# Attention's output projection in two halves with a PSUM bank of its own, and three PSUM banks instead of four for the values

## The chip, the cores and the metric

The kernel runs on one core of a Trainium2 chip. The metric is the time of one execution on the device in microseconds (us); lower is better. The core's engines are called as the profile calls them: PE is TensorE (PEld its weight loads), DVE is VectorE, ACT is ScalarE, POOL is GpSimd and SP is SyncE. PSUM, where matmuls write, has eight banks, each of 512 fp32 numbers on 128 partitions.

## The reference, cut to what matters

The input is an image of 256 x 256 places with 32 channels. Four layers follow one another, each of the form x = x + f(group_norm(x)): a gated attention, two Sobel filters (smoothing, two gradients, the root of the sum of their squares) and a recurrent network of two cells over 256 steps. The change lies in the first layer:

```python
mn = (m - mu) * jax.lax.rsqrt(var + LN_EPS) * ln_gamma + ln_beta
v = (mn @ Wv).reshape(B, s, i, H, C)                 # 32 -> 256 channels
g = jax.nn.sigmoid(mn @ Wg).reshape(B, s, i, H, C)   # 32 -> 256 channels
a = jnp.einsum('bsihc,btihc->bstih', q, k) * C ** (-0.5)
a = jax.nn.softmax(a, axis=2)
o = g * jnp.einsum('bstih,bsihc->bsihc', a, v)
return o.reshape(B, s, i, H * C) @ Wo + bo           # 256 -> 32 channels
```

In the last einsum `a` is summed over t, over which the softmax sums to one, so that o = g * v: what has to be computed is v, g, their product, and the projection with Wo.

## The kernel before, in words

The whole image stays on the chip. `xa` holds it with 128 partitions (four neighbouring columns of the image x 32 channels), 64 blocks of 256 places; two blocks make a pair, one operand of 128 x 512. `xb` has the normalized input of the attention in the same layout. There are NST = 32 pairs, and the attention runs over them in the step variable i.

In a step, `u` takes two values, 2i and 2i + 1: the halves of the 256 channels of v and g. In each half there are four values of `j`, the column within the group of four, which are 32 partitions each. So a step has eight value matmuls (Wv, line 313, into `pv`) and eight gate matmuls (Wg, line 313, into `pg`), each with 32 rows of contraction, 128 output channels and 512 places: each takes one of four row parts of TensorE, and different parts can work side by side. A sigmoid on ACT (line 328) turns a gate into `sg`, and a multiply on DVE (line 331) makes the product `o` from a value in PSUM and its gate.

`together` emits a group of four matmuls, two values and then two gates for later values, on four different row parts; after them the two sigmoids and the two multiplies. A half of a step has two such groups, and a step four. The gates run ahead: the first group of a half makes the gates of the next half's j = 2, 3, the second those of j = 0, 1 of the half after that, as the loop below has it.

`project(i)` (lines 333 to 347) makes the output of step i from its eight products: four matmuls for each half of the 256 channels (line 337), each with 128 rows of contraction and 32 output channels, one for each 32 partitions of the result, summed over the two halves in one bank `po`. Then ACT adds the bias (line 345, into `r`), POOL adds it to `xa` (line 347), and, two steps later, DVE takes the statistics of the new `xa` for the next normalization (line 350).

The order of instructions on each engine is the order in which the program emits them (`manual_schedule`). The eight PSUM banks are split into two pools of four: `ps_v` for the values, and `ps_g` for the gates and `po`. A tile takes over a bank of its pool when what was in it before has been read.

```python
for i in range(NST):
    for u in (2 * i, 2 * i + 1):
        if i >= 3 and u % 2:
            statistics(i - 3)
        together([(u, 0), (u, 1)], [(u + 1, 2), (u + 1, 3)])
        together([(u, 2), (u, 3)], [(u + 2, 0), (u + 2, 1)])
    if i >= 1:
        project(i - 1)
```

After the loop come the projection of the last step, the last three statistics and the normalization for the Sobel layer.

Of the kernel before, what the change touches and what calls it, by code (L numbers as in the profile page):

```python
# [10 lines left out]
F32 = mybir.dt.float32  # L11
# [3 lines left out]
PSUM = bass.MemoryType.PSUM  # L15

S = 256
T = 256
C = 32
J = 4  # L20
NB = T // J
P = 128
# [36 lines left out]
def net_kernel(  # L59
# [20 lines left out]
    nc = tc.nc  # L80
# [47 lines left out]
    wo = cp.tile([P, D // P, C], F32, name="wo")  # L128
    nc.gpsimd.dma_start(out=wo, in_=w_o.rearrange("(k p) c -> p k c", p=P))

    NST = NB // 2
    one = eps_tile(1.0, "one")

    def table(func, after):

        t = small.tile([P, 1], F32, name="table")
        nc.scalar.activation(t, after, func, scale=0.0, bias=one)
# [56 lines left out]
    with tc.tile_pool(name="nat", bufs=3) as natp, tc.tile_pool(  # L194
        name="ps_in", bufs=4, space=PSUM
# [33 lines left out]
    def pair(t, k):  # L229
        return t[:, 2 * k : 2 * k + 2, :].rearrange("p b s -> p (b s)")  # L230

    with tc.tile_pool(name="ln", bufs=4) as lnp:
        rstd = lnp.tile([P, 2 * S], F32, name="rstd", bufs=1)
        with tc.tile_pool(name="ps_ln", bufs=6, space=PSUM) as ps_ln, tc.tile_pool(
            name="ps_var", bufs=1, space=PSUM
# [38 lines left out]
        with tc.tile_pool(name="ps_sp", bufs=8, space=PSUM) as ps_sp:  # L274
            for i, (k, g, ks) in enumerate(pairs):
# [4 lines left out]
                    lhsT=spread[rows, ks * J : (ks + 1) * J, :].rearrange("p j c -> p (j c)"),  # L280
                    rhs=rstd[rows, :],
                    start=True,
                    stop=True,
# [18 lines left out]
    stats = new_stats()  # L302
    with tc.tile_pool(name="at", bufs=3) as atp, tc.tile_pool(
        name="ps_g", bufs=4, space=PSUM
    ) as ps_g, tc.tile_pool(name="ps_v", bufs=4, space=PSUM) as ps_v:
        gates, gated = {}, {}

        def inner(w, u, j, ps):
            i, half = divmod(u, 2)
            k = pairs[i][0]  # L310
            rows = slice(j * C, (j + 1) * C)
            mn = xb[rows, 2 * k : 2 * k + 2, :].rearrange("p b s -> p (b s)")
            nc.tensor.matmul(  # L313
                ps, lhsT=w[rows, half * P : (half + 1) * P], rhs=mn, start=True, stop=True
            )
            return ps

        def together(values, gates_of):

            pvs = {k: inner(wv4, *k, ps_v.tile([P, 2 * S], F32, name="pv")) for k in values}  # L320
            pgs = {
                k: inner(wg4, *k, ps_g.tile([P, 2 * S], F32, name="pg"))
                for k in gates_of
                if k[0] < 2 * NST
            }
            for k, pg in pgs.items():
                gates[k] = sg = atp.tile([P, 2 * S], F32, name="sg", bufs=8)
                nc.scalar.activation(sg, pg, AF.Sigmoid)  # L328
            for k, pv in pvs.items():
                gated[k] = o = atp.tile([P, 2 * S], F32, name="o", bufs=17)  # L330
                nc.vector.tensor_mul(o, pv, gates.pop(k))  # L331

        def project(i):
            po = ps_g.tile([P, 2 * S], F32, name="pg")
            for half in range(2):
                for j in range(J):
                    nc.tensor.matmul(
                        po[j * C : (j + 1) * C, :],
                        lhsT=wo[:, half, :],
                        rhs=gated.pop((2 * i + half, j)),  # L340
                        start=half == 0,
                        stop=half == 1,
                    )
            r = atp.tile([P, 2 * S], F32, name="r", bufs=2)
            nc.scalar.activation(r, po, AF.Identity, bias=bo4)
            dst = pair(xa, pairs[i][0])
            nc.gpsimd.tensor_add(dst, dst, r)

        def statistics(i):
            nc.vector.bn_stats(stats[:, i, :], pair(xa, pairs[i][0]))  # L350

        with tc.manual_schedule():
            together((), [(0, j) for j in range(J)])
            together((), [(1, j) for j in range(2)])
# [3 lines that stand above are left out]
                        statistics(i - 3)  # L358
                    together([(u, 0), (u, 1)], [(u + 1, 2), (u + 1, 3)])
                    together([(u, 2), (u, 3)], [(u + 2, 0), (u + 2, 1)])  # L360
                if i >= 1:
                    project(i - 1)
            table(AF.Sqrt, one)
            for i in range(NST - 1, NST):
                project(i)
            for i in range(NST - 3, NST):
                statistics(i)
    lw = ctx.enter_context(tc.tile_pool(name="lw", bufs=1))
# [644 lines left out]
```

## Time and profile before

| what | value |
|---|---|
| median of 3 runs | 2829.04 us |
| lowest and highest run | 2828.97 and 2829.38 us |
| the profiled execution, its own time | 2832.39 us |
| its span, from the first to the last instruction | 2830.5 us |
| mean granted TensorE clock | 0.991 of full speed |
| busy in the span: PE, DVE, ACT, POOL | 2785.1, 2494.4, 2379.3, 1299.9 us |
| attention stage, first gate matmul to last addition on POOL | 103.5 to 325.1 us of the span |
| in 130 to 190 us: PE, DVE, ACT, POOL busy | 60.00, 49.04, 45.12, 11.45 us of 60 |
| in 190 to 250 us: PE, DVE, ACT, POOL busy | 60.00, 49.05, 45.12, 11.46 us of 60 |

A line of the profile gives an instruction group by source line, engine, operation, and output <- input by tile name, with the number of instructions; then busy time and mean duration in ns; then the idle time of the engine ahead of the group and what ended it. In the timeline a line gives the start, the length, and how many instructions are merged in it. Instructions of one engine overlap, since the end of one runs beside the beginning of the next: the distance between starts, not the duration, is what one costs in a row. A busy PE is not a PE at its peak. A matmul in fp32 shows as two instructions of the same line.

### The profile page before, as it was taken

To read this page: it belongs to the slowest core of one execution; us is meant where nothing else is said; L and a number is where in the kernel's file an instruction comes from. 1 tells how busy PE (TensorE), PEld (TensorE's weight loads), DVE (VectorE), ACT (ScalarE), POOL (GpSimd) and SP (SyncE) were. 2 spreads that over 40 slices of the span, in tenths; PEclk is the share of its full clock that TensorE was granted. 3 is DMA by queue.
4 is the path that set the end of the run, shared out by engine and by line. 5 is a ranking of instruction groups with operands and counts; after the bars stand their busy time and mean duration, and the time that the engine had idled before them with its cause. 6 is when DMAs were issued, how large, how long until landed. Compare 5 with 4: busy or idle time off the path is not lost.

```text
span 2830.5 us, 38940 instructions
## 1 busy us (share of the span) xinstructions
PE 2785.1 (98%) x9709; PEld 1051.1 (37%) x9709; DVE 2494.4 (88%) x7272; ACT 2379.3 (84%) x6980; POOL 1299.9 (46%) x1295
## 2 busy tenths in 40 slices
PE   7999999999999999999999999999999999999998
PEld 4433434343333333333333333333333333333332
DVE  6788798978999999999999999999999999999997
ACT  5677676768988888888888888888888888888887
POOL 2211375654444444444444444444444444444443
PEclk9899999999999999999999999999999999999999
DMA  3000000010000000000000000000000000000000
GB/s 136 1 1 1 16 1 1 1 23 6 16 12 12 12 12 12 12 12 12 12 14 12 12 12 12 12 12 12 12 12 12 12 12 14 16 15 12 5 5 8
DMA packets 94337, 38.41 MB, mean 14 GB/s; under 512 B 74852, under 2 KB 91269, under 8 KB 94104
## 3 DMA queue, kind: packets, MB, share of 16 engines
q1 hardware_dynamic: 92612, 34.61, 5.3%
q8 instruction: 82, 1.34, 0.2%
q14 instruction: 151, 1.24, 0.1%
q10 hardware_dynamic: 692, 0.93, 0.1%
q0 software_dynamic: 800, 0.30, 0.0%
HBM read 10.63 MB, written 8.39 MB: 7 GB/s over the span
## 4 chain that ended last, share of the span: by engine, by line
PE 76%; DVE 1%; ACT 0%; issue 0%; POOL 0%; DVEq 0%; POOLq 0%; ACTq 0%
PE zz L853 34%; PE zz L828 19%; PE zz L848 15%; PE pt L910 5%; PE px L933 1%; PE px L930 1%; DVE ve L866 0%; PE px L924 0%; POOL rs L869 0%; ACT sq L861 0%; ACT ga L842 0%; DVE c L890 0%; DVE h L905 0%; DVE fc L894 0%; DVE c L898 0%
## 5 line engine op out<-in xcount | busy, mean ns | idle before, releaser
L869 POOL TENSOR_TENSOR rs<-ve,mhalf 128x4 f32<-128x4 f32 x1024 | 1037.5, 1013 | 1153.5 <-DVE ve L866 1153.5
L853 PE MATMUL zz<-wc,hT 128*128 128x512 f32 x2040 | 1100.3, 621 | 0.5 <-DVE hT L914 0.5
L842 ACT ACTIVATE ga<-zz,rs 128x128 f32<-128x128 f32 x3072 | 927.1, 366 | 32.0 <-POOL rs L869 13.1
L866 DVE TENSOR_REDUCE ve<-sq 128x4 f32<-128x516 f32 x1024 | 707.2, 691 | 123.8 <-ACT sq L861 61.1
L861 ACT ACTIVATE sq<-zz 128x512 f32<-128x512 f32 x1024 | 609.4, 595 | 126.4 <-PE zz L853 116.1
L828 PE MATMUL zz<-fx,xt 33*128 33x512 f32 x2048 | 583.1, 642 | 0.5 <-DVE e L710 0.5
L853 PEld LDWEIGHTS zz<-wc,hT 128*128 128x128 f32 x2040 | 324.0, 188 | 554.3 <-DVE c L898 288.1
L848 PE MATMUL zz<-wc,hT 128*128 128x512 f32 x1024 | 525.0, 594 | 0.0
L902 ACT ACTIVATE th<-c 128x128 f32<-128x128 f32 x1024 | 318.1, 311 | 89.9 <-DVE c L898 80.8
L842 ACT ACTIVATE go<-zz,rs 128x128 f32<-128x128 f32 x1024 | 390.4, 381 | 0.0
L890 DVE TENSOR_TENSOR c<-ga 128x128 f32<-128x128 f32 x1024 | 295.8, 289 | 39.2 <-ACT ga L842 25.2
L910 PEld LDWEIGHTS pt<-ident,h 128*128 128x128 f32 x1024 | 142.8, 139 | 502.1 <-DVE h L905 501.5
L914 DVE COPY hT<-pt 128x128 f32<-128x128 f32 x1024 | 292.6, 286 | 26.0 <-PE pt L910 4.0
L910 PE MATMUL pt<-ident,h 128*128 128x128 f32 x1024 | 299.5, 292 | 8.1 <-DVE h L905 8.1
L905 DVE TENSOR_TENSOR h<-go,th 128x128 f32<-128x128 f32 x1024 | 291.9, 285 | 11.8 <-ACT th L902 1.5
L894 DVE TENSOR_TENSOR fc<-ga,c 128x128 f32<-128x128 f32 x1020 | 297.5, 292 | 0.6 <-ACT ga L842 0.6
L898 DVE TENSOR_TENSOR c<-c,fc 128x128 f32<-128x128 f32 x1020 | 288.1, 282 | 6.8
L828 PEld LDWEIGHTS zz<-fx,xt 33*128 33x128 f32 x2048 | 156.3, 185 | 258.9 <-ACT go L842 193.7
L331 DVE TENSOR_TENSOR o<-pv,sg 128x512 f32<-128x512 f32 x256 | 158.1, 681 | 43.6 <-PE pg L313 37.7
L848 PEld LDWEIGHTS zz<-wc,hT 128*128 128x128 f32 x1024 | 162.3, 198 | 70.8 <-issue 40.8
L328 ACT ACTIVATE sg<-pg 128x512 f32<-128x512 f32 x256 | 138.6, 599 | 31.4 <-PE pg L313 26.7
L313 PE MATMUL pv<-xb,wv 32*128 32x512 f32 x512 | 156.5, 620 | 0.0
(154 smaller groups left out, 2174.5 us busy)
## 6 DMA issues: line engine op xcount, KB each, us to landing
xt<-xa SPq DMA_DIRECT2D x256, 64.0 KB, 2.0
nat<-in_x_dram SPq DMA_DIRECT2D x16, 512.0 KB, 7.9
out_dram<-st SPq DMA_DIRECT2D x254, 32.0 KB, 1.6
wc<-in_L_conv_W_cell_dram SPq DMA_DIRECT2D x2, 512.0 KB, 4.4
kt<-in_consts_dram ACTq DMA_DIRECT2D x1, 832.0 KB, 5.8
wv<-in_L_conv_Wv_dram POOLq DMA_DIRECT2D x4, 32.0 KB, 5.1
wg<-in_L_conv_Wg_dram POOLq DMA_DIRECT2D x4, 32.0 KB, 6.7
gamma<-in_L_conv_ln_gamma_dram POOLq DMA_DIRECT2D x4, 0.1 KB, 5.9
```

What stands on the lines that cost most here:

```text
L828: nc.tensor.matmul(zz, lhsT=x, rhs=fx[rows, l, :], start=True, stop=l == 0 and t == 0)
L842: nc.scalar.activation(dst, gates(x, g), func, scale=scale)
L848: nc.tensor.matmul(get("zz"), lhsT=v["hT", 0, t][:, seqs], rhs=wc[:, l, 0, :], start=False, stop=t == 0)
L853: nc.tensor.matmul(get("zz"), lhsT=v["hT", l, t - 1][:, seqs], rhs=wc[:, l, 1, :], start=False, stop=True,)
L861: nc.scalar.activation(sqs[l, h][:, :, 0:H], four(get("zz")), AF.Square, scale=float(H**-0.5))
L866: nc.vector.tensor_reduce(ve, sqs[l, h], AX.X, ALU.add)
L869: nc.gpsimd.tensor_tensor(rs, get("ve"), inputs.mhalf, ALU.pow)
L890: nc.vector.tensor_mul(c, gates(get("ga"), 0), gates(get("ga"), 3))
L894: nc.vector.tensor_mul(fc, gates(get("ga"), 1), get("c"))
L902: nc.scalar.activation(th, get("c"), AF.Tanh)
L910: nc.tensor.transpose(pt[:, 0:P], get("h"), ident)
L914: nc.vector.tensor_copy(v["hT", l, t][:, seqs], get("pt")[:, 0:P])
```

## The change

Three things are changed. `project` takes a half as its second argument: the first call for a step takes the tile `po` and emits the four matmuls of the first half, and the second call emits the other four and then the addition of the bias and the addition to `xa`. The calls stand inside the loop over `u`, each behind the two groups of that half of the next step. The tile `po` comes from a pool of its own, `ps_o`, with one bank, and `ps_v` has three banks instead of four; `ps_g` keeps four, which now serve gates alone.

```diff
     with tc.tile_pool(name="at", bufs=3) as atp, tc.tile_pool(
         name="ps_g", bufs=4, space=PSUM
-    ) as ps_g, tc.tile_pool(name="ps_v", bufs=4, space=PSUM) as ps_v:
+    ) as ps_g, tc.tile_pool(name="ps_v", bufs=3, space=PSUM) as ps_v, tc.tile_pool(
+        name="ps_o", bufs=1, space=PSUM
+    ) as ps_o:
...
-        def project(i):
-            po = ps_g.tile([P, 2 * S], F32, name="pg")
-            for half in range(2):
-                for j in range(J):
-                    nc.tensor.matmul(
-                        po[j * C : (j + 1) * C, :],
-                        lhsT=wo[:, half, :],
-                        rhs=gated.pop((2 * i + half, j)),
-                        start=half == 0,
-                        stop=half == 1,
-                    )
+        def project(i, half):
+
+            if half == 0:
+                gated["po"] = ps_o.tile([P, 2 * S], F32, name="po")
+            po = gated["po"]
+            for j in range(J):
+                nc.tensor.matmul(
+                    po[j * C : (j + 1) * C, :],
+                    lhsT=wo[:, half, :],
+                    rhs=gated.pop((2 * i + half, j)),
+                    start=half == 0,
+                    stop=half == 1,
+                )
+            if half == 0:
+                return
             r = atp.tile([P, 2 * S], F32, name="r", bufs=2)
             nc.scalar.activation(r, po, AF.Identity, bias=bo4)
...
                     together([(u, 0), (u, 1)], [(u + 1, 2), (u + 1, 3)])
                     together([(u, 2), (u, 3)], [(u + 2, 0), (u + 2, 1)])
-                if i >= 1:
-                    project(i - 1)
+                    if i >= 1:
+                        project(i - 1, u % 2)
             table(AF.Sqrt, one)
-            for i in range(NST - 1, NST):
-                project(i)
+            for half in range(2):
+                project(NST - 1, half)
```

## The prediction

> **What bounds the kernel now.** I read the page first, then the waits, then the order of time of one step of the attention stage. The page's fifth part names the stage's evictions and what they wait for:
>
> ```profile
> L331 DVE TENSOR_TENSOR o<-pv,sg 128x512 f32<-128x512 f32 x256 | 158.1, 681 | 43.6 <-PE pg L313 37.7
> L328 ACT ACTIVATE sg<-pg 128x512 f32<-128x512 f32 x256 | 138.6, 599 | 31.4 <-PE pg L313 26.7
> L313 PE MATMUL pv<-xb,wv 32*128 32x512 f32 x512 | 156.5, 620 | 0.0
> ```
>
> The multiplies on DVE cost most and idle only 43.6 us in the whole stage. The waits between 130 and 318 us say what stands against what:
>
> ```profile
> PEld pv L313 <- DVE o L331: 61.4, 113, 0.8
> DVE o L331 <- PE pg L313: 34.1, 28, 1.2
> ACT sg L328 <- PE pg L313: 22.5, 55, 0.5
> ```
>
> DVE waits 1.2 us once per step i (28 times in 28 steps). TensorE waits four times per step (113) until a multiply has freed a bank for a value. The timeline shows both, here one step's lines out of their neighbours:
>
> ```profile
> 205.44 0.70 PE L313 MATMUL pv<-xb,wv 32*128 32x512 f32 x2
> ...
> 206.67 2.48 DVE L331 TENSOR_TENSOR o<-pv,sg 128x512 f32<-128x512 f32 x4 [1.22 <-PE pg L313]
> ...
> 207.42 0.29 PEld L313 LDWEIGHTS pv<-xb,wv 32*128 32x128 f32 x2 [0.75 <-DVE o L331]
> 207.42 1.29 PE L313 MATMUL pv<-xb,wv 32*128 32x512 f32 x3
> 208.01 0.18 PEld L313 LDWEIGHTS pv<-xb,wv 32*128 32x128 f32 x1 [0.30 <-DVE o L331]
> 208.02 0.19 PEld L313 LDWEIGHTS pg<-xb,wg 32*128 32x128 f32 x2
> 208.02 0.70 PE L313 MATMUL pg<-xb,wg 32*128 32x512 f32 x2
> ...
> 209.22 0.70 PE L313 MATMUL pg<-xb,wg 32*128 32x512 f32 x2
> ...
> 209.67 2.47 DVE L331 TENSOR_TENSOR o<-pv,sg 128x512 f32<-128x512 f32 x4
> ...
> 210.28 1.92 PE L337 MATMUL pg<-o,wo 128*32 128x512 f32 x16
> 210.73 0.13 PEld L337 LDWEIGHTS pg<-o,wo 128*32 128x32 f32 x4 [0.30 <-issue]
> 211.16 0.13 PEld L337 LDWEIGHTS pg<-o,wo 128*32 128x32 f32 x4 [0.30 <-issue]
> ...
> 212.13 0.70 PE L313 MATMUL pv<-xb,wv 32*128 32x512 f32 x2
> ```
>
> Call a step's four groups A, B, C, D, and the values in each 1 and 2. A's values start at 205.44 and the next step's A at 212.13: a period of 6.69 us. DVE starts a multiply every 0.60 us (two runs of four from 206.67 to 209.07, where the statistics start, 0.60 us more until 209.67), so its nine instructions are 5.4 us; the rest is the stall of 1.22 us. The stall is TensorE's lump: D's gates start at 209.22, the projection at 210.28 and holds the array until 212.13, and DVE has used up what was banked. A matmul is two instructions (512 records for 256 evictions), each a round of 0.43 us (210.73 to 211.16); four matmuls on four parts of the array run side by side, so the projection is four rounds.
>
> The bank rule is read from 207.42: C's first value starts 0.75 us after the multiply of A's first began, that is when its reading (0.68 us) ends. C1 is the fourth value after A1, and there are four banks: they are taken in turn. And the order rule from 208.01: C's gates need no bank that was late (A's sigmoids were over), and yet load 0.01 us behind C's second value. What stands behind a waiting value on TensorE waits too.
>
> **What the Trainium skill says.** "PSUM — Partial Sum Buffer", section "Engine vs sequencer instructions", has matmuls start and complete in program order; the trace agrees where it matters, in C's gates at 208.02. "TensorEngine Tiling (Array Packing)", "Key Properties", says that a change of tiling mode drains TensorE; the groups use 32*128 tiles and the projection 128*32. The trace agrees and prices it: from 211.16 the projection has two rounds left, which end at 212.02, and the next group starts at 212.13, 0.11 us later. "TensorE: Matmul & The Clock Gate", "What's actually happening", has the clock halved after an idle window of some 3.4 us. The trace has one such window in this stage, 316.9 to 320.3 us with a granted 0.50, but after 3.4 us of value matmuls alone, not of idleness. I use that for a rival.
>
> **The change, part by part.**
>
> Nothing is added or removed in arithmetic: as many matmuls, multiplies, sigmoids, additions and statistics, no DMA. Two things move.
>
> *The split.* Each half is two rounds, behind B and behind D. The second half stays where the whole was. A half needs products that are at least a step old, so it waits for no multiply. Alone, with four banks for values, this would shorten the lump: A 0.53 + 0.43 (weights exposed, 205.44 to 205.98 to 206.41), B 0.86, drain 0.09, half 0.88, switch 0.11, thus 2.9 us per half step of TensorE, 5.8 us per step beside 5.4 of DVE.
>
> *The third bank.* A value now takes the bank of the third value before it. With groups of two, A's values take two banks, B1 the third, and B2 needs A1's. A1's multiply cannot have ended: A was issued only just before. So TensorE stands at B2, and behind it B's two gates, the half projection, and the next A. All of that is in one ring:
>
> 1. A's start to A1's multiply: 205.44 to 206.67, 1.23 us.
> 2. that multiply to the start of the value that takes its bank: 206.67 to 207.42, 0.75 us.
> 3. a second value that has waited for its bank, with its gates, to the projection: D's at 209.22 to 210.28, 1.06 us.
> 4. half a projection and the switch to the next group: 210.28 to 212.13 is 1.85 us for four rounds, less two of 0.43, 0.99 us.
>
> The sum is 4.03 us per half step, 8.06 us per step, against 6.69 now: 1.38 us more (6.685 by many periods). In term 1 nothing can be saved, for DVE is idle when A1 comes: its four multiplies of a half take 2.4 us, or 3.0 with the statistics, out of 4.03. Both edits together are thus worse than either cause suggests: the split halves the lump, but puts it twice behind a wait.
>
> Count. From step 1's A to step 31's there are 30 periods: 30 x 1.38 = +41.4 us. Step 0 has no projection; there the ring is terms 2, 0.96 us of B's gates on the rows that the next A's values need, and 0.43 + 0.69 to the multiply: 2.83 us per half, 5.67 against 4.79 (by DVE's starts, 108.30 to 113.09), +0.9. After step 31's A, the chain to the last r is 4.03 + 0.75 + 1.06, 1.2 to the eviction r of projection 30, 0.74 until r has freed the single bank that projection 31 now waits for, and four rounds with the step to r, 2.0: 9.8 us against 9.5 now (313.64 to 323.13). The present one holds the window at half clock, which cost about 1.3 us; with one in the new tail, +1.6, without, +0.3: I take +1. Sum: 41.4 + 0.9 + 1.0 = +43.3 us.
>
> *Costed at nothing.* The eviction r: ACT has eight sigmoids at 0.50 us and one r at 0.7, 4.7 us of 8.06, and r's bank is needed again only after A and B, two us later. Addition on POOL: 1.27 us per step. Statistics read a step two periods old. Four banks for gates alone, where po no longer rotates through them: the wait for r (5.3 us over 27 times) goes, at most 0.1 us a step and not in the ring. SP and POOL queues issue nothing in the stage that moves. Later stages see the same data at the same distance.
>
> Bounds of what isn't shown. The trace never has a single bank reused by projections, nor a half projection: the ring's terms could each be off by 0.05 us, which is 0.2 per half step at most and 12 us in all; either sign.
>
> This profiled execution took 2832.39 us, 1.9 more than its span and 3.35 over the median of the runs. On its own time the sum gives 2875.7, on the median 2829.04 + 43.3 = **2872.3 us**.
>
> **The rivals.**
>
> *Faster: the lump was the cost and the third bank is none.* For it: the 1.22 us stall per step is due to the lump of 1.85. Against: four waits per step for a bank already with four banks. It decides on one point: whether B2's bank is free when B1 goes. If it were, the period would be the 5.8 us above, 30 x (6.69 - 5.82) = -26 us: 2803. It would need a bank free before A1's multiply, 1.23 us after A's start, and B is due at 0.97. Chance 0.05.
>
> *The clock falls.* In 313.5 to 316.9 one or two of four row parts were at work and the next 3.4 us were granted half the clock, with rounds of 0.85 us. In the ring B1 runs alone for 0.86 of 4.03 us, yet the other rounds are full: 24 row rounds of 0.43 in 4 x 4.03 us, 0.64, where that stretch had some 0.35 (11 rounds in 4 x 3.4 us). Were a third of the ring's windows so throttled, its six rounds would cost 2.6 us more in each of 21 halves, +54: about 2926. Chance 0.06.
>
> *The ring is looser.* If the gates or the next group's values slip past the waiting value, term 3 falls by up to 0.5 us per half: 43 - 31 = +12, 2841. Against it stand C's gates. Chance 0.05, and 0.02 that all cancels within 0.2%.
>
> **How the numbers follow.** The ring has 0.82, and its own range is 2864 to 2881. About 0.2% is what a measurement of this kernel can tell from no change. Faster 0.05, same 0.02, slower 0.93. The range, 2861 to 2885, takes in the bound of the terms and leaves out the rivals.
>
> **What would show it.** A1's multiplies 8.06 us apart, with statistics in every second half; DVE's idle time before o near 85 us (8.06 - 5.4 = 2.7 per step, mostly before A1 and C1); value weights waiting for o about two times a step, not four, with gates and projection behind them; the sigmoid of B's gates late by the same. The stage ends near 367 us. Wrong if the period is under 6.7, if A's values wait for a bank, if PEclk drops in the stage, or if any later stage changes its length.

## The result, and the profile after

The changed kernel takes 2873.43 us (median of 4 runs, 2871.99 to 2875.87), the kernel before 2829.21 in the same comparison: a ratio of 1.0155, 95% interval 1.0138 to 1.0173, 44.2 us slower. 2872.3 had been forecast. The profiled execution took 2872.99 us, with a span of 2871.2.

The page of the changed kernel has the evictions of the stage two lines further down in the source (DVE's idle time is the last part):

```profile
L333 DVE TENSOR_TENSOR o<-pv,sg 128x512 f32<-128x512 f32 x256 | 165.1, 687 | 78.8 <-PE pg L315 66.8
L330 ACT ACTIVATE sg<-pg 128x512 f32<-128x512 f32 x256 | 138.7, 595 | 96.4 <-PE pg L315 96.1
L315 PE MATMUL pv<-xb,wv 32*128 32x512 f32 x512 | 196.7, 626 | 0.8 <-DVE o L333 0.8
```

DVE's idle time rises from 43.6 to 78.8 us and ACT's from 31.4 to 96.4, with the same instruction counts: neither has more to do, both wait longer. The waits from 130 to 358 us (28 steps; us in total, times, longest):

```profile
PEld pv L315 <- DVE o L333: 93.2, 113, 0.8
ACT sg L330 <- PE pg L315: 87.3, 112, 1.1
DVE o L333 <- PE pg L315: 61.2, 56, 1.4
```

DVE now waits twice per step, ACT four times. Where, the timeline shows: the end of one half step and the whole of the next, from its A at 207.78 to the following half's at 211.91.

```profile
205.72 0.18 PEld L315 LDWEIGHTS pv<-xb,wv 32*128 32x128 f32 x1 [0.81 <-DVE o L333]
205.73 0.19 PEld L315 LDWEIGHTS pg<-xb,wg 32*128 32x128 f32 x2
...
206.79 1.06 PE L341 MATMUL po<-o,wo 128*32 128x512 f32 x8
...
207.78 0.70 PE L315 MATMUL pv<-xb,wv 32*128 32x512 f32 x2
...
209.01 2.67 DVE L333 TENSOR_TENSOR o<-pv,sg 128x512 f32<-128x512 f32 x4 [1.37 <-PE pg L315]
...
209.76 0.18 PEld L315 LDWEIGHTS pv<-xb,wv 32*128 32x128 f32 x1 [0.81 <-DVE o L333]
209.83 0.18 PEld L315 LDWEIGHTS pg<-xb,wg 32*128 32x128 f32 x1
209.86 0.70 PE L315 MATMUL pg<-xb,wg 32*128 32x512 f32 x2
...
210.92 1.07 PE L341 MATMUL po<-o,wo 128*32 128x512 f32 x8
...
211.59 0.68 DVE L356 BATCH_NORM_STATS2 stats<-xa 128x6 f32<-128x512 f32 x1
211.91 0.19 PEld L315 LDWEIGHTS pv<-xb,wv 32*128 32x128 f32 x2 [0.84 <-DVE o L333]
```

That is the ring of the prediction: A's start to its multiply 1.23 us, the multiply to B's second value 0.75 (209.01 to 209.76), that value to the projection 1.16 (to 210.92), the half projection and the switch 0.99 (to 211.91). In the half step before, the third term, from 205.72 to 206.79, is 1.07 us.

### The profile page after: what moved, and what is told of

It reads as the page before. It is cut to its first block, busy times and chain, and to the rows that moved or that the text cites. A ratio compares the mean times of both kernels' runs of the same rounds, so it can differ in the third digit from the quotient of the medians.

```text
span 2871.2 us, 38940 instructions
## 1 busy us (share of the span) xinstructions
PE 2826.7 (98%) x9709; PEld 1043.3 (36%) x9709; DVE 2504.7 (87%) x7272; ACT 2374.7 (83%) x6980; POOL 1298.2 (45%) x1295
## 4 chain that ended last, share of the span: by engine, by line
PE 76%; DVE 0%; ACT 0%; issue 0%; POOL 0%; DVEq 0%; POOLq 0%; ACTq 0%
PE zz L859 34%; PE zz L834 19%; PE zz L854 15%; PE pt L916 5%; PE px L939 1%; PE px L936 1%; PE px L930 0%; POOL rs L875 0%; DVE ve L872 0%; ACT ga L848 0%; ACT sq L867 0%; DVE h L911 0%; DVE c L896 0%; DVE fc L900 0%; DVE c L904 0%
## 5 line engine op out<-in xcount | busy, mean ns | idle before, releaser
L333 DVE TENSOR_TENSOR o<-pv,sg 128x512 f32<-128x512 f32 x256 | 165.1, 687 | 78.8 <-PE pg L315 66.8
L330 ACT ACTIVATE sg<-pg 128x512 f32<-128x512 f32 x256 | 138.7, 595 | 96.4 <-PE pg L315 96.1
L315 PE MATMUL pv<-xb,wv 32*128 32x512 f32 x512 | 196.7, 626 | 0.8 <-DVE o L333 0.8
```

## The experiments

Each kernel ran beside runs of the kernel before on its chip; the ratios are to those. "As changed" is the kernel after, in which each edit is made unless the whole is named.

### e1: the split, with four banks for the values

```diff
-    ) as ps_g, tc.tile_pool(name="ps_v", bufs=3, space=PSUM) as ps_v, tc.tile_pool(
-        name="ps_o", bufs=1, space=PSUM
-    ) as ps_o:
+    ) as ps_g, tc.tile_pool(name="ps_v", bufs=4, space=PSUM) as ps_v:
...
-                gated["po"] = ps_o.tile([P, 2 * S], F32, name="po")
+                gated["po"] = ps_g.tile([P, 2 * S], F32, name="pg")
```

> The split alone: four banks for the values, po in the gates' pool of four as before, each half projection where the change puts it. The ring theory: B's second value takes a bank that was freed long ago, TensorE paces the first half of a step (2.9 us), DVE with the statistics the second (3.0 us), 5.96 us per step instead of 6.69, thus -22 us, about 2807 us. Rival, that the split itself costs the time (two more changes of tiling, 0.2 us each per step): 30 x 0.4 = +12 us or more, 2841 or above.

Measured: 2834.71 us, ratio 1.0018 (1.0011 to 1.0025). Neither: 5 us slower where 22 us less was expected by the ring, and 12 more by its rival. The period is 6.92 us. Its timeline has one half as calculated and one that is not:

```profile
205.49 0.70 PE L313 MATMUL pv<-xb,wv 32*128 32x512 f32 x2
...
207.48 1.06 PE L339 MATMUL pg<-o,wo 128*32 128x512 f32 x8
...
208.47 0.70 PE L313 MATMUL pv<-xb,wv 32*128 32x512 f32 x2
...
209.72 1.57 ACT L328 ACTIVATE sg<-pg 128x512 f32<-128x512 f32 x3 [0.92 <-PE pg L313]
...
210.36 0.29 PEld L313 LDWEIGHTS pg<-xb,wg 32*128 32x128 f32 x2 [0.72 <-ACT sg L328]
...
211.41 0.16 PEld L339 LDWEIGHTS pg<-o,wo 128*32 128x32 f32 x8 [0.76 <-issue]
...
212.41 0.70 PE L313 MATMUL pv<-xb,wv 32*128 32x512 f32 x2
```

The first half (205.49 to 208.47) takes 2.98 us. In the second (208.47 to 212.41, 3.94 us), D's second gate loads only at 210.36, after 0.72 us behind a sigmoid: C's first, at 209.72. The reason that suggests itself: `po` is taken behind B and freed only after D's projection, so that through C and D the gates have three banks, and a gate meets a ring like the values' one. e5 and e7 test this.

### e5: the missing bank taken from the gates

```diff
-        name="ps_g", bufs=4, space=PSUM
-    ) as ps_g, tc.tile_pool(name="ps_v", bufs=3, space=PSUM) as ps_v, tc.tile_pool(
+        name="ps_g", bufs=3, space=PSUM
+    ) as ps_g, tc.tile_pool(name="ps_v", bufs=4, space=PSUM) as ps_v, tc.tile_pool(
```

> The changed kernel with the missing bank taken from the gates: four banks for the values, three for the gates, one for po. The ring theory: B's second gate now waits for the sigmoid of A's first, which starts 1.21 us after A and frees the bank 0.66 us later; with 1.06 and 0.99 behind it 3.92 us per half, 7.84 per step, +35 us, 2865 us. Rival, that only the multiplies on DVE are slow enough to hold a bank: like the split with four and four, about 2807 us.

Measured: 2865.38 us, ratio 1.0126 (1.0110 to 1.0143); period 7.88 us. Its timeline, values in plenty and gates late:

```profile
205.11 0.70 PE L315 MATMUL pv<-xb,wv 32*128 32x512 f32 x2
...
207.00 0.29 PEld L315 LDWEIGHTS pg<-xb,wg 32*128 32x128 f32 x2 [0.72 <-ACT sg L330]
...
208.05 0.16 PEld L341 LDWEIGHTS po<-o,wo 128*32 128x32 f32 x8 [0.76 <-issue]
...
209.05 0.70 PE L315 MATMUL pv<-xb,wv 32*128 32x512 f32 x2
```

1.89 us until a gate's bank is free, 1.05 to the projection, 1.00 for it: 3.94 us, in both halves. It is the very duration of e1's slow half. Three banks are too few for either tile; who empties them, DVE or ACT, changes 0.1 us.

### e2: the third bank alone

```diff
-                    if i >= 1:
-                        project(i - 1, u % 2)
+                if i >= 1:
+                    for half in range(2):
+                        project(i - 1, half)
```

> The third bank alone: the whole projection behind D, three banks for values, po with its own bank. The ring theory: the half with the projection is 1.23 + 0.75 + 1.06 + 1.85 = 4.89 us; in the other the statistics stand between B's second multiply and C's first, which is 1.97 + 0.60 + 0.60 = 3.17 us after A's. 8.06 per step, +42 us, 2872 us: as slow as both edits together. Rival, that the two edits add up: without the split's -22 us the bank alone must cost 44 + 22 = +66 us, 2895.

Measured: 2873.41 us, ratio 1.0154 (1.0137 to 1.0171); period 8.06. The third bank alone is as slow as both edits together, and the additive rival (2895) is out. Its timeline:

```profile
206.57 2.67 DVE L333 TENSOR_TENSOR o<-pv,sg 128x512 f32<-128x512 f32 x4 [2.23 <-PE pg L315]
...
209.15 0.68 DVE L356 BATCH_NORM_STATS2 stats<-xa 128x6 f32<-128x512 f32 x1
...
209.75 2.65 DVE L333 TENSOR_TENSOR o<-pv,sg 128x512 f32<-128x512 f32 x4
```

From A's multiply to C's 3.18 us, with no idle time of DVE before the statistics or C's multiply. The trace has B's second multiply, which waited for its bank, 1.97 us behind A's; the statistics and then C's multiply follow it on DVE, 0.60 us each. The other half has the lump, 4.88 us with 2.23 us of idle time. In steps 1 and 2, which have no statistics, the same trace has DVE's starts only 7.80 and 7.73 us apart.

### e3: the same, with the statistics ahead of A

To e2's edit comes this one:

```diff
-                    if i >= 3 and u % 2:
+                    if i >= 3 and u % 2 == 0:
```

> The third bank alone, with the statistics ahead of A instead of C, where DVE waits for the projection anyway. The ring theory: the half without the projection is then 0.75 + 0.96 + 1.12 = 2.83 us instead of 3.17, and the step 4.89 + 2.83 = 7.72 us, against 8.06 with the statistics ahead of C: about -10 us to e2, 2863 us. Rival, that the ring is TensorE's alone and DVE's order does not count: 2873 as e2.

Measured: 2865.43 us, ratio 1.0126 (1.0111 to 1.0141), 8 us under e2, each against its own runs of before; DVE's starts are 7.80 and 7.73 us apart in turn. So in e2 the statistics are on the path, as expected.

### e6: the changed kernel, with the statistics ahead of A

The edit is e3's, to the changed kernel as it is.

> The changed kernel with the statistics ahead of A instead of C. The ring theory: DVE waits in both halves, 0.8 us or more beside the statistics, so their place costs nothing: 8.1 us per step, 2873 us as changed. Rival, that DVE's statistics delay a multiply that frees a bank: about -10 us, 2863, as between the two kernels with the whole projection.

Measured: 2874.80 us, ratio 1.0159 (1.0143 to 1.0174), the changed kernel's 1.0155. With the split, DVE has time to spare in both halves, and where its statistics stand costs nothing. Beside e3, which ran against the same runs of before and differs from it only in the split, e6 is 9.4 us slower: with three banks and the statistics out of the way, the split costs time.

### e4: the half projection between the two groups

```diff
                     together([(u, 0), (u, 1)], [(u + 1, 2), (u + 1, 3)])
+                    if i >= 1:
+                        project(i - 1, u % 2)
                     together([(u, 2), (u, 3)], [(u + 2, 0), (u + 2, 1)])
-                    if i >= 1:
-                        project(i - 1, u % 2)
```

> The changed kernel with each half projection between the two groups of its half instead of behind the second. The ring theory: every second value waits for the multiply of the group before, wherever the projection stands, so the ring has the same four terms (the next A's second value waits for B's first multiply): 8.06 to 8.12 us per step, 2873 us as changed. Rival, that the projection's place behind B's waiting value is the cost: it would now cover that wait, 3.03 us per half, 6.06 per step, about 2810 us.

Measured: 2872.95 us, ratio 1.0149 (1.0132 to 1.0166); period 8.07. One half from its D to the next step's B:

```profile
205.50 0.70 PE L315 MATMUL pv<-xb,wv 32*128 32x512 f32 x2
...
206.72 2.67 DVE L333 TENSOR_TENSOR o<-pv,sg 128x512 f32<-128x512 f32 x4 [0.96 <-PE pg L315]
...
207.47 0.18 PEld L315 LDWEIGHTS pv<-xb,wv 32*128 32x128 f32 x1 [0.81 <-DVE o L333]
...
208.53 1.06 PE L341 MATMUL po<-o,wo 128*32 128x512 f32 x8
...
209.53 0.70 PE L315 MATMUL pv<-xb,wv 32*128 32x512 f32 x2
```

The load at 207.47 is that of A's second value, which waits for D's first multiply at 206.72; the terms are 1.22, 0.75, 1.06 and 1.00 us. Moving the projection out from behind B's waiting value gains nothing, since it then stands in front of B, and the second value of the next group, C or A, waits for the first multiply of B or D. It is not the place behind a certain group that costs, but that with three banks some second value always waits for the first multiply of the group before, and the projection is in the ring wherever it stands.

### e7: two evictions, so that no bank is held

To e1's edit comes this one: each half projection takes its own bank, is evicted at once and added to `xa` by POOL. The arithmetic is the reference's, summed in another order.

```diff
-            if half == 0:
-                gated["po"] = ps_g.tile([P, 2 * S], F32, name="pg")
-            po = gated["po"]
+            po = ps_g.tile([P, 2 * S], F32, name="pg")
...
-                    start=half == 0,
-                    stop=half == 1,
+                    start=True,
+                    stop=True,
                 )
-            if half == 0:
-                return
             r = atp.tile([P, 2 * S], F32, name="r", bufs=2)
-            nc.scalar.activation(r, po, AF.Identity, bias=bo4)
+            if half == 0:
+                nc.scalar.copy(r, po)
+            else:
+                nc.scalar.activation(r, po, AF.Identity, bias=bo4)
```

> The split with four value banks and four banks for gates and po, where each half projection has its own bank and its own eviction: the half is no longer summed in PSUM but added to xa by POOL, one more ACT copy and one more POOL addition per step. In e1 po kept one of the four banks from B to the end of D, and D's second gate waited for C's sigmoid (3.94 us for that half of the step against 2.99 for the other). If that held bank is the cause, both halves now take 2.9 to 3.0 us: 5.97 us per step, -21 us, about 2808 us. Rival, that the split is slow in itself, by its changes of tiling or the second half's place: the period stays at 6.9 and the time at 2834 or more, with ACT's additional copy on top.

Measured: 2809.83 us, ratio 0.9927 (0.9914 to 0.9941), 20.1 us under the kernel before: faster than both. The period is 5.98 us. The timeline has no late gate any more:

```profile
207.22 0.70 PE L313 MATMUL pv<-xb,wv 32*128 32x512 f32 x2
...
208.45 2.48 DVE L331 TENSOR_TENSOR o<-pv,sg 128x512 f32<-128x512 f32 x4 [0.44 <-PE pg L313]
...
209.28 1.06 PE L337 MATMUL pg<-o,wo 128*32 128x512 f32 x8
...
210.28 0.70 PE L313 MATMUL pv<-xb,wv 32*128 32x512 f32 x2
...
210.47 0.59 ACT L346 COPY r<-pg 128x512 f32<-128x512 f32 x1
...
210.85 0.68 DVE L353 BATCH_NORM_STATS2 stats<-xa 128x6 f32<-128x512 f32 x1
...
211.50 1.89 DVE L331 TENSOR_TENSOR o<-pv,sg 128x512 f32<-128x512 f32 x3
```

The halves take 3.06 us (207.22 to 210.28) and 2.92 us. DVE's stall per step has shrunk from 1.22 to 0.44 us. The additional copy and addition lie beside other work. Thus, with four banks for values, the split comes near the 5.8 us per step that the prediction gave it alone, and meets e1's expectation of 5.96, but only if the bank in which it sums is not kept across two groups: that is what e1 lacked.

## Why the prediction was right

The ring was right in its mechanism and nearly in its size. Step by step:

- **Term 1, term 2 and term 4** measured 1.23, 0.75 and 0.99 us after, as forecast.
- **Term 3** was mis-sized: it came out at 1.07 us in most half steps, where 1.06 was forecast, but at 1.16 in every fourth. DVE's starts give a step of 8.17 and 8.07 us in turn, mean 8.12, where 8.06 was forecast. In the slow half above, the loads of the two gates stand 0.08 us apart from the value's (209.76, then 209.83), and a semaphore instruction of 51 ns stands there, 18 of them in the stage. "Perfetto Trace Analysis", section "Identifying Dependency Chains", in the Trainium skill says that such instructions may be put ahead of one that waits for several engines; here they fall 16.24 us apart, on the slow steps. In e4, where they fall beside the projection, the period is 8.07 throughout. That is a reading of two traces; no run takes them away alone.
- **The count.** From the first multiply to the next layer's scale (the activation `std`), the stage took 220.3 us before and 265.0 after, +44.7, by DVE's and ACT's starts in both traces. Of it, 30 periods are 243.6 - 200.5 = +43.0 (forecast +41.4), step 0 is 5.68 - 4.79 = +0.9 (forecast 0.9), and the tail +0.8 (forecast 1). That last agreement is in part luck: the forecast was a middle between +1.6 with a half clock in the new tail and +0.3 without. No half clock fell into the changed kernel's stage, and the tail still grew by 0.8: the chain from step 31's A to the last r took 10.0 us instead of 9.8, and the rest lies behind it. The two profiled spans differ by less, 40.7 us: the changed execution came to the stage 2.4 us earlier and had the layers behind it 1.6 us shorter, in code that the edit leaves alone, and so by the look of it a difference of two executions.
- **The rivals.** The clock stayed at full speed from 102 us to the end of the stage, so the clock's rival is out. A looser ring is out too: behind the waiting value at 209.76 the gates load only at 209.83, and term 3 is no shorter than forecast. The faster rival's pace of 5.8 us was not to be had by a fourth bank alone: e1 has one and needs 6.92. The step that failed there is "Alone, with four banks for values, this would shorten the lump": it left out that `po`, once split, holds one of the gates' four banks through C and D. The changed kernel's own bank for `po` does avoid that, and pays with the values' fourth. The kernel's eight banks are one too few for four, four and a held one.
- **A wait was misread.** Four waits of value weights for a multiply were read in the waits of before as four waits for a bank, and two were forecast for after; there are four again (113 in 28 steps). One of them per projection, such as that at 211.91 with 0.84 us, is the load behind the projection, named by the last semaphore although the multiplies that freed the banks of its two values, the second and third of the four from 209.01, were over at 210.90. So two of after's four are for a bank, and three of before's.
- **The idle time.** 85 us were forecast before `o`, 78.8 came; 0.77 to 0.87 and 1.37 us before the two halves' first multiplies. The forecast took 0.60 us for every instruction, the distance of two starts; an idle time counts from the end of a multiply, 0.68 us or more behind its start.
- **The order.** The ring needs only that nothing passes a matmul that waits for a bank, and in the timeline after nothing does. Program order is not strict where nothing waits: the trace of before has B's gates start at 206.41, 13 ns ahead of B's values, which the program emits first.

In short, what the change does is explained by the third bank. With the whole projection it costs 43 us (e2), and with the split 44; the split gives back nothing there, since it shortens a lump that stands once in the ring by placing it there twice. That the two are so nearly equal is a coincidence: in e2 the statistics add what the split adds in the changed kernel. Without that, as e3 and e6 have it, the whole projection takes 7.77 us per step and the split 8.12.

## What to carry to other kernels

Count the ring before a bank is taken away: with n banks a tile waits for the eviction of the n-th before it, and all that the matmul queue has behind that tile, here gates, a projection and two switches of tiling, becomes part of a serial loop. A partial sum that is kept open across other groups takes a bank from them for the whole time, and closing it early with one more eviction on engines that have time to spare can be cheaper, as e7 is beside e1. Moving such work to another place in the queue helps only if it leaves the ring.

## What the runs showed of the hardware that was not expected

A semaphore instruction of 51 ns ahead of a gate's weights seems to cost a step 0.10 us when it falls where TensorE has just been waiting, and nothing elsewhere (e4), with 18 of them in either stage; why 0.10 us and not 51 ns, no run shows. Three banks for values give 4.03 us per half (e4, 205.50 to 209.53) and three for gates 3.94 (e5), though DVE takes 0.68 us for an eviction and ACT 0.60: most of a ring is not the eviction but the way to it and back.
